# A graph layer on one core: more columns picked by VectorE and ScalarE, segments summed in half the width, and VectorE's picks placed last in each step

## The chip, the cores and the metric

The kernel runs on one core of a Trainium2 chip. The core has five engines, each with its own in-order stream of instructions: TensorE (PE, with its weight loads as PEld), VectorE (DVE), ScalarE (ACT), GpSimd (POOL) and SyncE (SP), which issues DMAs. A name with a q behind it (DVEq) means the engine's sequencer, which reads the stream and does register work itself. The metric is the device time of one execution in microseconds (us), as a median of several runs.

## The reference, cut to what matters

A graph network layer over 12,500 nodes of 128 features and 412,500 edges, sorted by target node `dst`, followed by a residual and a layer norm:

```python
f0, f1 = x0 @ W1_0e, einsum('nui,uw->nwi', x1, W1_1o)      # feat | self, scaled
e0, e1 = feat0[edge_src], feat1[edge_src]                   # gather by source node
h = gelu(gelu(edge_scalar_attr @ W_mlp1) @ W_mlp2)          # 8 -> 64 -> 64, per edge
w00, w01, w10, w11 = h @ Wp_00, h @ Wp_01, h @ Wp_10, h @ Wp_11
out0_a = w00 * e0 * ea0;            out0_b = w11 * sum(e1 * ea1)
out1_a = (w01 * e0) x ea1;          out1_b = w10 * e1 * ea0
n0, n1 = segment_sum(mid0, edge_dst), segment_sum(mid1, edge_dst)
y = c * self + s * (n0 @ W2_0e, n1 @ W2_1o)
out = layernorm(x + y)
```

All in fp32. `edge_attr_4` is (ea0, ea1), `edge_attr_8` is edge_scalar_attr.

## The kernel before, in words

Edges go in 806 runs of 512 (128 partitions, Q = 4 groups); four runs make a chunk (CH = 4), so there are 201.5 chunks. Before the main loop, the kernel turns x into `xT` (nodes along the free axis, kept in SBUF) and writes the projected features `table` to DRAM.

The rows of source nodes reach a run's tile `G` in four ways. Most are GpSimd's indirect DMAs, one for each group of 128 edges (`gather`, L194). The first RAW = 16 runs gather rows of x itself, since the table is not ready, and TensorE and ScalarE project them (`turn_rows`, `features`). Every 14th run, SP fetches one group row by row (`aid`, L184). And VectorE and ScalarE *pick*: an engine loads the node numbers of some edges as addresses into its registers (L154), then copies one column of `xT` for each (L165 on DVE, L167 on ACT) into a tile `gt`; when 128 columns are there, a matmul with `wf` (L173) and an eviction by ScalarE (L174) put them into `G`. `COLS` says how many runs one picked group takes: 5 on DVE and 7 on ACT. `gather` runs 19 runs ahead (LEAD = 20).

For each run, VectorE multiplies edge weights and gathered rows into `M` (messages, three instructions: L538 once, L541 twice). TensorE multiplies `M` by the selection `S` (32 columns: 4 attributes x 8 target nodes) into `seg`, 32 x 256 for each group (segments, L550), and ScalarE evicts all 256 columns (L553). A placing matrix `pl` (VectorE, L559, one for each run) says at which of 32 nodes of a window each segment belongs; `place` multiplies (L566 and L567), and `add` (L577) adds each run's window to the accumulator `acc` on VectorE at an offset loaded into a register (L572). `select` builds `oh` and `S` for the next chunk (L525, L529). Groups of 512 finished nodes, about one in eight chunks, go through `moments` (L594 to L607) and, two groups at a time, `normalise` (L614 to L625).

The order of PE, ACT, DVE and SP is written out by hand, in the loop over steps s at the end of the function; c, k = divmod(s, 4) are the chunk and the step in it. On VectorE a step is: messages of run s, its placing matrix, the register load and the copies of its picks; then, at k = 2, `add` for the chunk before; at k = 3 `norm` and then `select` for the next chunk; in other steps one piece of clearing (L365) if any is due. An instruction that needs a result waits on a semaphore in its place; the additions to `acc` wait for one another and S for oh.

Of the kernel before, what the change touches and what calls it, by code (L numbers as in the profile page):

```python
# [20 lines left out]
P = 128  # L21
# [15 lines left out]
LEAD = 20  # L37
RAW = 16
MARGIN = 64
# [5 lines left out]
STEPS = 12  # L45
COLS = {DVE: 5, ACT: 7}
COL_Q = {DVE: Q - 2, ACT: Q - 3}
# [5 lines left out]
def gnn_kernel(ctx: ExitStack, tc: tile.TileContext, x, src, dst, ea4, ea8, w1_0, w1_1, wm1, wm2,  # L53
# [54 lines left out]
    for e, per in COLS.items():  # L108
        picked[e], (t, k) = [], COL_TURN[e]
        while True:  # L110
            at = t + per + 1
            at += (k - at) % CH
            if at + 2 >= NS - 1:
                break
            picked[e].append((t, at, at + 2))
            t += per
    pick_of = {(e, s): i for e, g in picked.items() for i, (_, _, s) in enumerate(g)}
# [7 lines left out]
    def aid_load():  # L125


        nc.sync.dma_start(aid_at, sub(src, AID_FROM * SB + (Q - 1) * P, [[AID * SB, len(aided)], [1, P]]))
        nc.vector.tensor_scalar(aid_at, aid_at, float(4 * P), None, op0=OP.mult)
        for e, g in picked.items():  # L130
            cycle = CH // math.gcd(CH, COLS[e])
            for h in range(0, len(g), P):
                part = g[h:h + P]
                rows = cst.tile([len(part), P], I32, name=f"pick{len(pick_rows)}")
                for i in range(min(cycle, len(part))):
                    n = len(part[i::cycle])
                    nc.sync.dma_start(rows[i::cycle], sub(src, part[i][2] * SB + COL_Q[e] * P,
                                                          [[cycle * COLS[e] * SB, n], [1, P]]))
                nc.vector.tensor_scalar(rows, rows, 4.0, float(x_at), op0=OP.mult, op1=OP.add)
                for i in range(len(part)):  # L140
                    pick_rows[e, h + i] = rows[i:i + 1]
# [3 lines left out]
    def pick_nodes(e, s):  # L145

        per = COLS[e]
        i, t = divmod(s - COL_TURN[e][0], per)
        if not 0 <= i < len(picked[e]):
            return  # L150
        if t == 0:
            GT[e, i] = wk.tile([P, P], F32, name=f"gt{list(picked).index(e)}", bufs=3)
# [34 lines left out]
    def gather(s):  # L187
        b, c = divmod(s, P)
        G[s] = wk.tile([P, Q, P], F32, name="G", bufs=LEAD)
        for q in range(Q):  # L190
            if q == Q - 1 and s in aided or any(q == COL_Q[e] and (e, s) in pick_of for e in picked):
                continue
# [88 lines left out]
    wpost = cst.tile([P, 4, P], F32)  # L281
    ones = cst.tile([P, 1], F32)

    def line(dtype=F32):
# [9 lines left out]
    def clear():  # L294
        nc.vector.memset(wpost, 0.0)
        nc.vector.memset(ones, 1.0)
        nc.vector.memset(odd, 0.0)

    def weight_loads():
# [89 lines left out]

    raws = {}  # L390

    def load_raws(b):
        raws[b] = [load_run_rows(dst, b, NO_NODE), load_run_rows(src, b, 0)]

    def load_indices(b):
# [4 lines left out]
        for kind, raw in zip((1, 0), raws.pop(b)):  # L400
            f = wk.tile([P, SB], F32, name="rawf")
            nc.vector.tensor_copy(f[:ns, :], raw[:ns, :])
            if kind:
                g = wk.tile([P, SB], F32, name="rawr", bufs=1)
                off = against_window(f, g, ns)
# [14 lines left out]

    def load_run_rows(a, b, fill):
        ns = min(P, NS - b * P)
        part = b * P + ns == NS and REM < SB
        fl = ns - 1 if part else ns
        raw = wk.tile([P, SB], I32, name="raw")
        if part:
# [6 lines left out]

    e4, e8, eT, H1, H2, WP, S, M, PL, SG, ST = {}, {}, {}, {}, {}, {}, {}, {}, {}, {}, {}

    def load_edges(b):
        s0 = b * CH
        ns = min(CH, NS - s0)
        e4[b] = wk.tile([P, CH, Q, 4], F32, name="e4", bufs=EDGES_AHEAD)
        e8[b] = wk.tile([P, CH, Q, RAD], F32, name="e8", bufs=EDGES_AHEAD)  # L440
        part = s0 + ns == NS and REM < SB
        fl = ns - 1 if part else ns
        if part:
            nc.vector.memset(e4[b][:, fl], 0.0)
        if fl < CH:
            nc.vector.memset(e8[b][:, fl:], 0.0)
        for a, t, n in ((ea8, e8[b], RAD), (ea4, e4[b], 4)):
            if fl:
                nc.sync.dma_start(t[:, :fl].rearrange("p s q k -> p (s q) k"),
                                  sub(a, s0 * SB * n, [[n, P], [P * n, fl * Q], [1, n]]))  # L450
            if part and RQ:
                nc.sync.dma_start(t[:, fl, :RQ, :], sub(a, (s0 + fl) * SB * n, [[n, P], [P * n, RQ], [1, n]]))
            if part and RP:
                nc.sync.dma_start(t[:RP, fl, RQ, :], sub(a, ((s0 + fl) * SB + RQ * P) * n, [[n, RP], [1, n]]))

# [64 lines left out]
    def select(c):  # L520

        n = min(CH, NS - c * CH)
        b, r = divmod(c * CH, P)
# [3 lines left out]
                                .to_broadcast([P, n, Q, J]), op=OP.is_equal)  # L527
        S[c] = wk.tile([P, CH * Q, 4, J], F32, name="S")
        nc.vector.tensor_tensor(S[c][:, :n * Q],  # L529
                                oh[:, :n].rearrange("p s q j -> p (s q) j")[:, :, None, :]  # L530
                                .to_broadcast([P, n * Q, 4, J]),
                                e4[c][:, :n].rearrange("p s q k -> p (s q) k")[:, :, :, None]
                                .to_broadcast([P, n * Q, 4, J]), op=OP.mult)

# [10 lines left out]
    def segments(s):  # L545

        c, r = divmod(s, CH)
        pt = ps.tile([P, 2 * P], F32, name="seg", bufs=1)
        for q in range(Q):
            nc.tensor.matmul(pt[q * W:(q + 1) * W, :], S[c][:, r * Q + q].rearrange("p k j -> p (k j)"),  # L550
                             M[s][:, q].rearrange("p a u -> p (a u)"), start=True, stop=True)
        SG[s] = wk.tile([P, 2 * P], F32, name="sg", bufs=CH + 2)
        nc.scalar.activation(SG[s], pt, AF.Copy)  # L553

    def placing(s):

        b, r = divmod(s, P)
        PL[s] = wk.tile([P, P], F32, name="pl", bufs=CH + 1)
        nc.vector.tensor_scalar(PL[s], iota, colv[b][:, r:r + 1], None, op0=OP.is_equal)  # L559

    def place(c):
        ns = min(CH, NS - c * CH)
        ST[c] = pt = ps.tile([P, CH, 4, W], F32, name="m", bufs=1)
        for k in range(ns):
            s = c * CH + k
            nc.tensor.matmul(pt[:, k, 0, :], SG[s][:, :P], PL[s][:, :W], start=True, stop=True)  # L566
            nc.tensor.matmul(pt[:, k, 1:, :].rearrange("p a n -> p (a n)"), SG[s][:, P:], PL[s][:, W:],  # L567
                             start=True, stop=True)

# [12 lines left out]
    def moments(b, sums=None):  # L582
# [6 lines left out]
        pend.append(b)  # L589
        pt = ps.tile([P, XB, P], F32, name="m", bufs=1)  # L590
        st = wk.tile([P, XB, 6], F32, name="bst")
# [16 lines left out]

    def normalise():
        y, mv = Y["y"], Y["v"]  # L610
# [11 lines left out]
        for j, b in enumerate(pend):  # L622
            for t, k in group(b)[4]:
                i = j * XB + t
                nc.scalar.activation(y[:k, j, t, :], y[:k, j, t, :], AF.Identity,  # L625
                                     bias=m[:k, i:i + 1], scale=r[:k, i:i + 1])
# [3 lines left out]
    def norm(bs, last=False):  # L630
        for b in bs:
            moments(b)
            if not last:
                move_sums()
                new_sums()
            if len(pend) == LNB:
                normalise()
        if last and pend:
            normalise()

# [116 lines left out]
    with tc.manual_schedule(engines={PE, ACT, DVE, SP}):  # L757
# [7 lines left out]
        for b in range(min(3, NG)):  # L765
# [3 lines left out]
        loads = list(weight_loads())  # L769
        extra = {2: lambda: load_edges(0), 4: lambda: load_raws(0), NG // 2: lambda: load_indices(0),  # L770
                 NG // 2 + 3: make_w1b, NG // 2 + 5: make_ws, NG - 6: lambda: radial(0), NG - 4: lambda: mlp1(0),
# [36 lines left out]
        for s in range(NCH * CH + CH):  # L808
# [7 lines left out]
            if s % P == P // 2 and (s // P + 1) * P < NS:  # L816
                load_indices(s // P + 1)
            for t in range(P // ROWS):
                a = s + AID_LEAD - t * STEPS // (P // ROWS)
# [11 lines left out]
            if k == (0 if end else 1) and 0 < c <= NCH:  # L831
                place(c - 1)
            for e in picked:
                if (e, s + 2) in pick_of:
                    picked_rows(e, pick_of[e, s + 2])
            if k > 1 and c + 2 < NCH:
                pick(ACT, P)
                (mlp1 if k == 2 else mlp2)(c + 2)
            pick(ACT, P)
            pick_nodes(ACT, s + 1)  # L840
            if s + 1 < raw_runs:
                turn_rows(s + 1)
            if s < NS:
                messages(s)
                placing(s)
                pick_nodes(DVE, s)
                pick(DVE, P)
            if s + 1 < raw_runs:
# [3 lines left out]
            if k == (1 if end else 3) and 0 < c <= NCH:  # L852
                norm(due.get(c - 1, []), last=c == NCH)
                clearing += [(c, a) for a in range(4)] if c - 1 in due and c < NCH else []
            elif clearing:
                clear_sums(clearing.pop(0)[1])
            if k == 3 and c + 1 < NCH:
                select(c + 1)
            if s == NS - 8:
                count_odd()  # L860
# [31 lines left out]
```

## Time and profile before

| | |
|---|---|
| median of 10 runs | 3692.02 us (3686.87 to 3697.24) |
| the profiled execution | 3693.36 us |
| its span in the profile | 3691.6 us |
| mean granted clock of TensorE | 0.786 |
| gathers on GpSimd (L194) | 2835 from the table, 64 from x |
| picks | 20224 columns on DVE, 14336 on ACT |
| DMA | 244.14 MB, 990429 packets, 896838 of them under 512 B |

The page of the profile gives for each engine its busy time, share of the span and number of instructions, and for each group of instructions (line, engine, operation, output <- inputs, count) the busy time, the mean ns of one, the idle time just before them and what ended most of it. "issue" is idle time in which an engine waited for nothing that the profile shows. The view of waits sums the same idle times: total us, how often, longest.

### The profile page before, as it was taken

What the parts mean: (1) busy time and instruction counts of PE and PEld (TensorE: products, weight loads), DVE (VectorE), ACT (ScalarE), POOL (GpSimd) and SP (SyncE); (2) the same over time, 40 slices, a digit from 0 to 9 for tenths busy, and PEclk for the clock granted to TensorE, in tenths of its full rate; (3) what the DMA queues carried; (4) which work ended last, traced back from release to release, by engine and by line L of the source; (5) the groups of instructions that cost most, each with busy time, mean ns of one, the idle gap of its engine ahead of it and who ended that gap; (6) DMA issues with size and microseconds to landing.
All of it is one profiled execution on the core that took longest, in us unless ns stands there. A gap on an engine that the chain in (4) does not pass through costs nothing.

```text
span 3691.6 us, 117877 instructions
## 1 busy us (share of the span) xinstructions
PE 2864.8 (78%) x24857; PEld 2032.4 (55%) x24857; DVE 3062.0 (83%) x25248; ACT 2277.7 (62%) x16665; POOL 2763.7 (75%) x2906
## 2 busy tenths in 40 slices
PE   5688777778778778778778788777787877787787
PEld 4555555555555555555555455555555555555555
DVE  3698898889799888888887888878888888788886
ACT  2366676666566666666666566666566666566654
POOL 6777777777777777777777777777777777777775
PEclk8887888778778787787777777778777778777776
DMA  8233333333333333333333333333333333333331
GB/s 201 55 57 66 66 61 61 61 68 66 60 66 62 61 67 67 61 67 61 60 66 67 60 65 62 62 66 66 62 61 66 61 62 65 62 61 65 61 62 48
DMA packets 990429, 244.14 MB, mean 66 GB/s; under 512 B 896838, under 2 KB 941705, under 8 KB 989699
## 3 DMA queue, kind: packets, MB, share of 16 engines
q0 software_dynamic: 92768, 190.17, 19.3%
q1 hardware_dynamic: 876673, 39.90, 14.4%
q10 hardware_dynamic: 20258, 6.46, 0.7%
q14 instruction: 532, 4.36, 0.4%
q8 instruction: 198, 3.24, 0.4%
HBM read 223.49 MB, written 12.80 MB: 64 GB/s over the span
## 4 chain that ended last, share of the span: by engine, by line
DVE 32%; PE 15%; issue 14%; POOL 12%; DMA 9%; SPq 8%; DVEq 5%; ACT 5%; ACTq 0%; POOLq 0%
DVE gt L165 14%; POOL G L194 12%; DVE M L541 8%; DMA G<-table,idx 7%; SPq L184 5%; DVEq L154 4%; DVE M L538 3%; PE seg L550 2%; PE w L499 2%; PE m L567 2%; DVE acc L577 2%; PE m L597 2%; DVE pl L559 2%; SPq L180 2%; PE m L566 2%
## 5 line engine op out<-in xcount | busy, mean ns | idle before, releaser
L194 POOL DMA_INDIRECT G<-table,idx x2835 | 2702.2, 953 | 881.2 <-issue 734.7
L165 DVE COPY gt<-xT 128x1 f32 x20224 | 1301.6, 144 | 241.8 <-issue 230.3
L167 ACT ACTIVATE gt<-xT 128x1 f32 x14336 | 1448.4, 192 | 37.0 <-issue 34.0
L550 PE MATMUL seg<-M,S 128*32 128x256 f32 x6448 | 628.6, 468 | 489.3 <-DVE M L541 381.9
L541 DVE TENSOR_TENSOR M<-w,G 128x384 f32<-128x384 f32 x1580 | 798.6, 547 | 0.0
L499 PE MATMUL w<-wpb,h 64*128 64x128 f32 x6448 | 714.1, 355 | 106.2 <-DVE M L541 105.0
L553 ACT ACTIVATE sg<-seg 128x256 f32<-128x256 f32 x806 | 305.8, 379 | 741.4 <-PE seg L550 665.8
L499 PEld LDWEIGHTS w<-wpb,h 64*128 64x128 f32 x6448 | 591.5, 248 | 243.0 <-DVE M L541 132.6
L567 PE MATMUL m<-pl,sg 128*128 128x96 f32 x1612 | 505.3, 410 | 0.0
L550 PEld LDWEIGHTS seg<-M,S 128*32 128x32 f32 x6448 | 144.5, 118 | 624.3 <-issue 245.5
L538 DVE TENSOR_TENSOR M<-w,G 128x256 f32<-128x256 f32 x790 | 323.5, 410 | 135.4 <-DMA G<-table,idx 85.5
L566 PEld LDWEIGHTS m<-pl,sg 128*128 128x128 f32 x1612 | 358.7, 275 | 117.8 <-issue 111.6
L566 PE MATMUL m<-pl,sg 128*128 128x32 f32 x1612 | 383.9, 327 | 5.6 <-ACT sg L553 3.8
L567 PEld LDWEIGHTS m<-pl,sg 128*128 128x128 f32 x1612 | 372.3, 284 | 0.0
L482 PE MATMUL h<-h,w2b 64*64 64x256 f32 x3232 | 314.2, 403 | 51.8 <-ACT h L471 49.0
L467 PEld LDWEIGHTS h<-eT,w1b 64*128 64x128 f32 x3232 | 270.8, 250 | 148.5 <-issue 139.3
L467 PE MATMUL h<-eT,w1b 64*128 64x128 f32 x3232 | 314.9, 351 | 8.7 <-ACT eT L460 8.7
L174 ACT ACTIVATE G<-h 128x128 f32<-128x128 f32 x270 | 74.1, 274 | 345.2 <-PE h L173 303.2
L482 PEld LDWEIGHTS h<-h,w2b 64*64 64x64 f32 x3232 | 139.6, 136 | 232.2 <-ACT h L471 186.7
L577 DVE TENSOR_TENSOR acc<-m,acc 128x128 f32 x806 | 234.1, 290 | 33.6 <-PE m L567 2.4
L471 ACT ACTIVATE h<-h 128x512 f32<-128x512 f32 x404 | 217.6, 590 | 63.8 <-PE h L467 61.3
L559 DVE TENSOR_SCALAR pl<-iota,colv 128x128 f32<-128x128 f32 x806 | 236.7, 294 | 8.4 <-PE m L567 8.4
(109 smaller groups left out, 1692.4 us busy)
## 6 DMA issues: line engine op xcount, KB each, us to landing
G<-table SPq DMA_DIRECT2D x7040, 0.5 KB
G<-table,idx POOLq DMA_INDIRECT x2835
e<-in_edge_attr SPq DMA_DIRECT2D x201, 64.0 KB
e<-in_edge_attr SPq DMA_DIRECT2D x201, 32.0 KB
xt<-in_x SPq DMA_DIRECT2D x24, 256.0 KB
table<-ft ACTq DMA_DIRECT2D x24, 256.0 KB
out<-y SPq DMA_DIRECT2D x24, 256.0 KB
raw<-in_dst SPq DMA_DIRECT2D x6, 256.0 KB
```

Source lines behind the costliest of these rows:

```text
L165: nc.vector.tensor_copy(to, col)
L167: nc.scalar.activation(to, col, AF.Copy)
L194: nc.gpsimd.indirect_dma_start(out=G[s][:, q, :], out_offset=None, in_=x if s < raw_runs else table, in_offset=bass.IndirectOffsetOnAxis(a ...
L467: nc.tensor.matmul(p1[h][:, j // 2, j % 2, :], w1b[rows, j, :], eT[c][rows, :], start=True, stop=True)
L482: nc.tensor.matmul(p2[r][k * HID:(k + 1) * HID, h * n:(h + 1) * n], w2b[rows, :], H1[c][h][rows, k * n:(k + 1) * n], start=True, stop=True)
L499: nc.tensor.matmul(WP[i][:, q, :], H2[c][q % 2][rows, k, q // 2, :], wpb[rows, :], start=True, stop=True)
L538: nc.vector.tensor_tensor(m[:, :, :, :MUL], w[:, :, :2 * MUL].rearrange("p q (a u) -> p q a u", a=2), g[:, :, None, :MUL].to_broadcast([P, ...
L541: nc.vector.tensor_tensor(m[:, :, j, MUL:].rearrange("p q (i u) -> p q i u", i=3), w[:, :, None, (2 + j) * MUL:(3 + j) * MUL].to_broadcast ...
L550: nc.tensor.matmul(pt[q * W:(q + 1) * W, :], S[c][:, r * Q + q].rearrange("p k j -> p (k j)"), M[s][:, q].rearrange("p a u -> p (a u)"), s ...
L559: nc.vector.tensor_scalar(PL[s], iota, colv[b][:, r:r + 1], None, op0=OP.is_equal)
L566: nc.tensor.matmul(pt[:, k, 0, :], SG[s][:, :P], PL[s][:, :W], start=True, stop=True)
L567: nc.tensor.matmul(pt[:, k, 1:, :].rearrange("p a n -> p (a n)"), SG[s][:, P:], PL[s][:, W:], start=True, stop=True)
```

## The change

What differs, in the order of the diff:

- RAW 18 for 16; picks of one group in 4.5 runs on DVE (4 and 5 in turn) and 6 on ACT. `pick_nodes` spreads a group's 128 columns over the steps it has.
- Groups wholly past the last edge are cleared and not gathered.
- The four edge attributes come in rows of 128 edges, 2 KB each, for 32 runs at a time, and are turned by four transposes on TensorE and one eviction on ScalarE (`load_attributes`, `turn_attributes`). They came before with each chunk, 16 bytes a piece.
- `S` has 56 columns: 8 of attribute 0, 24 of zeros, 24 of attributes 1 to 3. Segments are two matmuls of 128 columns each into the same 128 columns, with columns 0 to 31 and then 24 to 55 of S. ScalarE evicts two runs in one instruction of 256 columns. `select` writes S in two instructions.
- `placing` makes the four matrices of a chunk in one instruction at k = 0; `place` is one matmul for each run.
- On VectorE the register load and copies of a step's picks come last in the step, behind `add`, `norm`, clearing and `select`. Clearing is done only at k = 1.
- `moments` uses another PSUM bank; group 0 is normalised alone, so the last pair is complete, and of that last pair every other tile is normalised by VectorE; a square root ahead of it loads ScalarE's table.
- Tiles of raw indices share other buffers.

```diff
-RAW = 16
+RAW = 18
-COLS = {DVE: 5, ACT: 7}
+COLS = {DVE: 4.5, ACT: 6}
...
     def pick_nodes(e, s):
-        per = COLS[e]
-        i, t = divmod(s - COL_TURN[e][0], per)
-        if not 0 <= i < len(picked[e]):
+        if (e, s) not in step_of:
             return
+        i, t = step_of[e, s]
+        per = len(picked[e][i][0])
...
         for q in range(Q):
+            if q * P >= E - s * SB:
+                nc.vector.memset(G[s][:, q, :], 0.0)
+                continue
...
+    def turn_attributes(b):
+        pt = ps.tile([P, 4, P], F32, name="h")
+        raw = e4_raw.pop(b).rearrange("t (e k) -> t k e", k=4)
+        for k in range(4):
+            nc.tensor.transpose(pt[:, k, :], raw[:, k, :], ident)
+        e4[b] = wk.tile([P, 4, P], F32, name="e4")
+        nc.scalar.activation(e4[b], pt, AF.Copy)
...
     def select(c):
...
-        nc.vector.tensor_tensor(S[c][:, :n * Q], ... op=OP.mult)
+        own = S_own[c % 2][:, :n * Q]
+        nc.vector.tensor_tensor(own[:, :, :J], hot, a[:, :, 0:1].to_broadcast([P, n * Q, J]), op=OP.mult)
+        nc.vector.tensor_tensor(own[:, :, W:].rearrange("p t (k j) -> p t k j", j=J),
+                                hot[:, :, None, :].to_broadcast([P, n * Q, 3, J]),
+                                a[:, :, 1:, None].to_broadcast([P, n * Q, 3, J]), op=OP.mult)
...
     def segments(s):
-        for q in range(Q):
-            nc.tensor.matmul(pt[q * W:(q + 1) * W, :], S[c][:, r * Q + q]..., M[s][:, q]..., start=True, stop=True)
-        nc.scalar.activation(SG[s], pt, AF.Copy)
+        for h, col in enumerate((0, W - J)):
+            for q in range(Q):
+                nc.tensor.matmul(SEG[c][q * W:(q + 1) * W, r, :], own[:, r * Q + q, col:col + W], M[s][:, q, h, :],
+                                 start=h == 0, stop=h == 1)
+        if r % 2 or s == NS - 1:
+            nc.scalar.activation(SG[c][:, r // 2 * 2:r + 1, :], SEG[c][:, r // 2 * 2:r + 1, :], AF.Copy)
-    def placing(s):
-        nc.vector.tensor_scalar(PL[s], iota, colv[b][:, r:r + 1], None, op0=OP.is_equal)
+    def placing(c):
+        nc.vector.tensor_tensor(PL[c][:, :n], iota[:, None, :].to_broadcast([P, n, P]),
+                                colv[b][:, r:r + n, None].to_broadcast([P, n, P]), op=OP.is_equal)
     def place(c):
-            nc.tensor.matmul(pt[:, k, 0, :], SG[s][:, :P], PL[s][:, :W], start=True, stop=True)
-            nc.tensor.matmul(pt[:, k, 1:, :]..., SG[s][:, P:], PL[s][:, W:], start=True, stop=True)
+            nc.tensor.matmul(pt[:, k]..., SG[c][:, k, :], PL[c][:, k, :], start=True, stop=True)
...
+                if last and t % 2:
+                    nc.vector.tensor_scalar(y[:k, j, t, :], y[:k, j, t, :], r[:k, i:i + 1], m[:k, i:i + 1],
+                                            op0=OP.mult, op1=OP.add)
+                    continue
-            if len(pend) == LNB:
-                normalise()
+            if len(pend) == LNB or b == 0:
+                normalise(last)
...
             if s < NS:
                 messages(s)
-                placing(s)
-                pick_nodes(DVE, s)
-                pick(DVE, P)
+                if k == 0:
+                    placing(c)
             if s + 1 < raw_runs:
                 features(s + 1)
             if k == (1 if end else 2) and 0 < c <= NCH:
                 add(c - 1)
             if k == (1 if end else 3) and 0 < c <= NCH:
                 norm(due.get(c - 1, []), last=c == NCH)
-            elif clearing:
+            elif k == 1 and clearing:
                 clear_sums(clearing.pop(0)[1])
             if k == 3 and c + 1 < NCH:
                 select(c + 1)
+            if s < NS:
+                pick_nodes(DVE, s)
+                pick(DVE, P)
```

## The prediction

> **What bounds the kernel now.** I read the busy shares first, then the waits, then the timeline of VectorE, which the chain of waits passes through most often (32%) without naming a limit.
>
> ```profile
> span 3691.6 us, 117877 instructions
> PE 2864.8 (78%) x24857; PEld 2032.4 (55%) x24857; DVE 3062.0 (83%) x25248; ACT 2277.7 (62%) x16665; POOL 2763.7 (75%) x2906
> ...
> L194 POOL DMA_INDIRECT G<-table,idx x2835 | 2702.2, 953 | 881.2 <-issue 734.7
> L165 DVE COPY gt<-xT 128x1 f32 x20224 | 1301.6, 144 | 241.8 <-issue 230.3
> ```
>
> From the waits:
>
> ```profile
> POOL G L194 <- issue: 753.9, 2472, 0.3
> ...
> DVE gt L165 <- issue: 230.3, 479, 1.7
> ...
> DVE M L538 <- DMA G<-table,idx: 85.5, 69, 6.3
> ...
> DVE M L538 <- DMA G<-table: 29.4, 7, 6.6
> ```
>
> GpSimd looks 75% busy, but its pauses are 2472 of at most 0.3 us, one behind nearly every gather: 0.95 + 0.30 us is its own rhythm. In the trace its 2899 gathers start from 3.5 to 3665.8 us, 1.264 us apart. **GpSimd is the bound.** VectorE is hardly behind: its only slack is what messages wait for gathered rows, 85.5 + 29.4 = 114.9 us. So VectorE by itself would need about 3691.6 - 114.9 = 3577 us, 3% less. Its 230 us of "issue" idle is no slack. The timeline of VectorE over one chunk of four runs (start, length, line, idle before) tells what it is:
>
> ```profile
> 1522.44 0.28 DVE L559 TENSOR_SCALAR pl<-iota,colv 128x128 f32<-128x128 f32 x1
> 1523.05 1.79 DVE L165 COPY gt<-xT 128x1 f32 x28 [0.33 <-issue]
> 1524.76 0.42 DVE L538 TENSOR_TENSOR M<-w,G 128x256 f32<-128x256 f32 x1
> 1525.09 1.01 DVE L541 TENSOR_TENSOR M<-w,G 128x384 f32<-128x384 f32 x2
> 1526.02 0.28 DVE L559 TENSOR_SCALAR pl<-iota,colv 128x128 f32<-128x128 f32 x1
> 1526.57 1.54 DVE L165 COPY gt<-xT 128x1 f32 x24 [0.27 <-issue]
> 1528.03 1.26 DVE L577 TENSOR_TENSOR acc<-m,acc 128x128 f32 x4
> 1529.20 0.41 DVE L538 TENSOR_TENSOR M<-w,G 128x256 f32<-128x256 f32 x1
> 1529.53 1.01 DVE L541 TENSOR_TENSOR M<-w,G 128x384 f32<-128x384 f32 x2
> 1530.46 0.28 DVE L559 TENSOR_SCALAR pl<-iota,colv 128x128 f32<-128x128 f32 x1
> 1531.34 1.78 DVE L165 COPY gt<-xT 128x1 f32 x28 [0.60 <-issue]
> 1533.05 0.28 DVE L525 TENSOR_TENSOR oh<-iota,rel 128x128 f32<-128x128 f32 x1
> 1533.36 0.69 DVE L529 TENSOR_TENSOR S<-oh,e 128x512 f32<-128x512 f32 x1
> ```
>
> Ahead of each group of copies the sequencer of VectorE loads their column addresses into registers (L154). The line's own view, for the time from 1529.2 to 1531.3:
>
> ```profile
> L154 DVEq TENSOR_LOAD <-pick x1: 1946/1946/1946, 1529.3 to 1529.3; - x1
> ```
>
> The copies begin 0.09 us after that load ends. Over the run a load of 24 takes 1.67 us and one of 28 takes 1.93 us, so 65 ns a register. The load costs nothing only as far as VectorE has work queued ahead of it; today that is messages and a placing matrix, 1.26 + 0.23 us.
>
> **The held sequencer.** Additions (L577) wait for one another, and S (L529) waits for oh (L525). In the trace the sequencer does nothing of its own while such an instruction waits: in none of 197 chunks does a sequencer instruction start between oh and S, and behind the last addition the next one starts 14 ns after that addition starts (197 of 198). A load put behind additions therefore begins when the fourth addition begins.
>
> The Trainium skill speaks against this: "Perfetto Trace Analysis", DVE / Act Engine Instruction, has a VectorE instruction wait in a queue of its own while the sequencer goes on. By that rule the moved load starts early and the first rival below comes true; the 14 ns above contradict it.
>
> **The change, part by part (VectorE, 201.5 chunks).**
>
> *More picks.* The built program has 2863 gathers, 36 fewer (36 x 1.264 = 45.5 us off GpSimd: 3646 if it stayed the bound), and 175 instead of 158 picks on VectorE. 17 x 128 = 2176 copies, 61 ns from start to start (four copies more are 0.24 us more in the timeline): **+133**.
>
> *Placing by chunk.* Four L559 of 0.23 us start to start go; one broadcast of 128x512 comes, which I price as L529, 0.61 us start to start. (0.61 - 0.92) x 201.5 = **-62**; between -93 (as short as L541's 0.46) and 0 (as long as the four).
>
> *Select in two pieces.* S of 0.61 us becomes 128x128 (0.23, like L559) and 128x384 (0.46, like L541): +0.08 x 201.5 = **+16**; between -30 (L541's 0.46 alone) and +62 (two of L541's, 0.92).
>
> *Clearing* moves to the second step of a chunk, whose idle (next) covers its 0.4 us, 100 times: **-41**.
>
> *Picks behind everything else.* The registers per step become 24, 28 or 32 (mean 28.4); a load takes 1.96 on average (32 by the slope: 2.19) and copies start 2.05 after the load starts. Messages occupy 1.26 us. The load usually starts 0.1 us before the messages do (median in the trace).
> - Step 0, messages and placing: copies could start at -0.10 + 2.05 = 1.95; the work ends at 1.26 + 0.61 = 1.87. Idle 0.08.
> - Step 1, messages alone: 1.95 - 1.26 = 0.69.
> - Step 2, messages and additions: these start 0.325 apart, the fourth at 1.26 + 3 x 0.325 = 2.24, and the work ends at 2.53. Load at 2.25, copies at 4.30. Idle 1.77.
> - Step 3, messages, then select: its first product starts at 1.26 + 0.32 = 1.58, the second is pushed 0.07 later, then the load: copies at 3.70; the work ends at 2.34. Idle 1.36.
>
> Sum 3.90 a chunk; 787 steps with picks are 196.75 chunks: 767 us, against 241.8 today: **+525**. All else queued on VectorE stands behind that load: the next messages, for which TensorE's segments wait, and through the freed buffers of G in the end GpSimd. Bounds of this term: with loads held nowhere it is 0.08 + 0.69 + 0.1 a chunk, 171 us, so -70; with no load running ahead of its step at all (step 0 and 1 start 0.2 us later) +600.
>
> *Moments in another bank, norm later.* L606 waits 64.5 us for ACT's copy of y; the additions are now about 1.2 us further ahead of it in each of 24 groups. Between 0 and -64; I take **-32**.
>
> *Start and end.* Twelve loads of pick indices take 9.16 us of SP; 20 are needed, +6 us, and VectorE waits for them; clearing the two S tiles about +2; the last normalise shared, with its table load ahead (1.28 us) and three pairs of tiles: -3. **+5**. 18 raw runs change little: the raw runs go at 5 us each, close to the new step.
>
> *Hidden.* TensorE sheds one of two placing matmuls a run (L566: 383.9 us) and ACT half its evictions of seg (L553: 305.8 us); in place of 16-byte pieces, attributes come in whole rows, with 4 transposes and one eviction each 32 runs. Neither engine nor the DMA engines (busy 3 tenths) set the end, so I count all at nothing. Without that cover, TensorE's new weight loads for segments (6448 more x 118 ns) are dearer by 144 us at most (L550, busy), less than it sheds. ACT gets 18 picks more at 12.9 us (1448.4 / 112); rival four.
>
> Sum: 3577 + 133 - 62 + 16 - 41 + 525 - 32 + 5 = 4121 us of span. The profiled execution took 3693.4, 1.8 more than its span, and the median of ten runs is 3692.0, so the two may be set equal: **4122 us**. A chunk then takes 20 us on VectorE against 14.2 gathers x 1.264 = 17.9 on GpSimd: the bound has passed to VectorE, and faster gathers are worth nothing.
>
> **Rivals.**
> 1. *The sequencer goes on while additions and products wait* (what would make it so: the 14 ns behind L577 being the wait of that next instruction itself). Idle is 171 us, VectorE needs 3577 + 133 - 62 + 16 - 41 - 70 - 32 + 5 = 3526, GpSimd keeps the end: 3646 + 2 = **3648, faster**. It decides if VectorE's chunk falls under 17.9, which needs over half of the 3.9 us hidden. For it: only that a pause of 14 ns is inferred, not labelled. Against: 197 of 197.
> 2. *Only one of two holds is real.* If the load gets past the additions but not past select, 1.65 us a chunk less: 4122 - 325 = **3797**. Against it: both show the same 14 ns.
> 3. *The loads are shorter than the slope says, or TensorE's relief ends small waits of VectorE*: a tenth off every load is 0.2 x 4 x 197 = 158: **3964**. Durations of one size vary only from 1.60 to 1.87, so little of that.
> 4. *ScalarE joins the chain.* It has 11.3 us busy a chunk now, 11.8 with the picks and fewer evictions, and four loads of 21 registers (1.35 each by its own 16 and 20: 1.05 and 1.29): 17.2 if nothing of them is hidden, under 20. If its waits for TensorE (0.5 to 1 us a step) add to that, a chunk becomes some 21.5: 4122 + 1.5 x 197 = **4418**.
>
> **How the numbers follow.** Forecast 84%; rival 1 7%, rival 2 3%, rival 3 as the lower end of the forecast's own range (counted in it), rival 4 5%, a change that leaves the time within 0.2% 1%. Range 3970 to 4260: from rival 3 to the forecast with loads not ahead at all (+75) and no gain at the norm or from clearing (+73); that leaves out about two in ten. 0.2% is about what measurement can tell from no change. Slower 92%, within 1%, faster 7%.
>
> **What will show it.** Right: VectorE's copies show "issue" idle near 770 us, longest in the steps behind additions (about 1.8) and select (about 1.4); pauses of GpSimd over 0.3 us become common and wait for VectorE's messages; messages wait for no gathers; L166's copies number 22400. Wrong: gathers still 1.264 us apart throughout (rival 1), or idle behind additions alone missing (rival 2), or ACT without pauses (rival 4).

## The result and the profile after

The changed kernel takes 4108.13 us (median of 8 runs, 4102.12 to 4118.56), the kernel before beside it 3692.87 us (28 runs). The ratio is 1.1127, with a 95% interval of 1.1118 to 1.1137: 415 us slower, 14 us under the forecast. The profiled execution took 4105.95 us with a span of 4104.1.

The page of the changed kernel, the same lines as before and one more (L198, L166 and L575 are L194, L165 and L538 of before):

```profile
span 4104.1 us, 131172 instructions
...
PE 2855.8 (70%) x29891; PEld 2117.8 (52%) x29891; DVE 3148.1 (77%) x27026; ACT 2410.7 (59%) x18631; POOL 2751.7 (67%) x2870
...
L198 POOL DMA_INDIRECT G<-table,idx x2791 | 2682.5, 961 | 1236.2 <-issue 772.4
L166 DVE COPY gt<-xT 128x1 f32 x22400 | 1430.1, 144 | 667.6 <-issue 656.3
...
L575 DVE TENSOR_TENSOR M<-w,G 128x256 f32<-128x256 f32 x788 | 325.9, 414 | 0.6 <-ACT G L175 0.2
```

Every engine is a smaller share of a longer span. That alone says that the time went into waiting. One copy still takes 144 ns; the idle time ahead of the copies went from 241.8 to 667.6 us, by 426, slightly more than the kernel lost. The messages, which waited 114.9 us for gathered rows, now wait 0.6 us for anything: they leave VectorE no slack. The waits (total us, times, longest) show who waits instead:

```profile
POOL G L198 <- issue: 793.5, 2516, 3.0
...
DVE gt L166 <- issue: 656.3, 515, 2.3
...
POOL G L198 <- DVE M L578: 355.5, 162, 17.0
...
DVE bst L648 <- ACT y L644: 112.0, 23, 8.1
...
PEld h L636 <- ACT h L521: 48.9, 23, 2.9
```

(The last two bear on the moments, in the section on the prediction.)

GpSimd keeps its rhythm (the median from gather to gather is 1.25 us) but stops 162 times, up to 17 us, until messages free a buffer of `G`; the mean from gather to gather becomes 1.401 us where it was 1.264. The bound has passed from GpSimd to VectorE.

VectorE's timeline in the changed kernel, the steps k = 2 and 3 of one chunk (start, length, line, idle before):

```profile
1520.98 0.41 DVE L575 TENSOR_TENSOR M<-w,G 128x256 f32<-128x256 f32 x1
1521.32 1.01 DVE L578 TENSOR_TENSOR M<-w,G 128x384 f32<-128x384 f32 x2
1522.24 1.26 DVE L619 TENSOR_TENSOR acc<-m,acc 128x128 f32 x4
1525.25 1.79 DVE L166 COPY gt<-xT 128x1 f32 x28 [1.74 <-issue]
1526.95 0.42 DVE L575 TENSOR_TENSOR M<-w,G 128x256 f32<-128x256 f32 x1
1527.28 1.01 DVE L578 TENSOR_TENSOR M<-w,G 128x384 f32<-128x384 f32 x2
1528.21 0.28 DVE L560 TENSOR_TENSOR oh<-iota,rel 128x128 f32<-128x128 f32 x1
1528.53 0.32 DVE L567 TENSOR_TENSOR S<-oh,e 128x128 f32<-128x128 f32 x1
1528.77 0.54 DVE L568 TENSOR_TENSOR S<-oh,e 128x384 f32<-128x384 f32 x1
1530.83 2.03 DVE L166 COPY gt<-xT 128x1 f32 x32 [1.52 <-issue]
```

And the view of the register load (L155) between 1522 and 1525.3 us (duration in ns, then when it starts):

```profile
L155 DVEq TENSOR_LOAD <-pick x1: 1934/1934/1934, 1523.2 to 1523.2; - x1
```

The four additions start at 1522.24 and every 0.325 us after it, so the fourth starts at 1523.2: there the load of 28 registers begins. It ends at 1525.15, and the copies start at 1525.25. VectorE's work ended at 1523.50; 1.74 us are lost in this step and 1.52 in the next.

### The profile page after: what moved, and what is told of

It is laid out like the page before. It is cut to its first block, busy times and chain, and to the rows that moved or that the text cites. A ratio compares the mean times of both kernels' runs of the same rounds, so it can differ in the third digit from the quotient of the medians.

```text
span 4104.1 us, 131172 instructions
## 1 busy us (share of the span) xinstructions
PE 2855.8 (70%) x29891; PEld 2117.8 (52%) x29891; DVE 3148.1 (77%) x27026; ACT 2410.7 (59%) x18631; POOL 2751.7 (67%) x2870
## 2 busy tenths in 40 slices
DMA packets 578334, 242.65 MB, mean 59 GB/s; under 512 B 481996, under 2 KB 526899, under 8 KB 577539
## 5 line engine op out<-in xcount | busy, mean ns | idle before, releaser
L198 POOL DMA_INDIRECT G<-table,idx x2791 | 2682.5, 961 | 1236.2 <-issue 772.4
L166 DVE COPY gt<-xT 128x1 f32 x22400 | 1430.1, 144 | 667.6 <-issue 656.3
L168 ACT ACTIVATE gt<-xT 128x1 f32 x16640 | 1662.9, 191 | 143.6 <-issue 141.8
L592 PE MATMUL seg<-M,S 128*32 128x128 f32 x12896 | 693.7, 343 | 497.5 <-DVE M L578 382.9
L592 PEld LDWEIGHTS seg<-M,S 128*32 128x32 f32 x12896 | 364.7, 129 | 697.5 <-issue 304.1
L595 ACT ACTIVATE sg<-seg 128x256 f32<-128x256 f32 x403 | 151.9, 377 | 700.9 <-PE seg L592 684.9
L610 PE MATMUL m<-pl,sg 128*128 128x128 f32 x1612 | 380.9, 410 | 1.3 <-ACT sg L595 1.3
L610 PEld LDWEIGHTS m<-pl,sg 128*128 128x128 f32 x1612 | 324.6, 299 | 69.9 <-issue 68.0
L575 DVE TENSOR_TENSOR M<-w,G 128x256 f32<-128x256 f32 x788 | 325.9, 414 | 0.6 <-ACT G L175 0.2
L619 DVE TENSOR_TENSOR acc<-m,acc 128x128 f32 x806 | 233.1, 289 | 23.5 <-PE m L610 2.1
L505 ACT ACTIVATE h<-h 128x512 f32<-128x512 f32 x404 | 216.0, 585 | 30.8 <-PE h L501 30.1
L521 ACT ACTIVATE h<-h 128x512 f32<-128x512 f32 x404 | 214.4, 581 | 14.8 <-PE h L516 9.1
L174 PE MATMUL h<-wf,gt 128*128 128x128 f32 x610 | 173.4, 382 | 7.6 <-DVE bst L648 7.6
L174 PEld LDWEIGHTS h<-wf,gt 128*128 128x128 f32 x610 | 157.2, 313 | 10.8 <-issue 10.8
```

Of the source, the lines that this page charges most:

```text
L166: nc.vector.tensor_copy(to, col)
L168: nc.scalar.activation(to, col, AF.Copy)
L174: nc.tensor.matmul(pt, GT.pop((e, i)), wf, start=True, stop=True)
L198: nc.gpsimd.indirect_dma_start(out=G[s][:, q, :], out_offset=None, in_=x if s < raw_runs else table, in_offset=bass.IndirectOffsetOnAxis(a ...
L575: nc.vector.tensor_tensor(m[:, :, :, :MUL], w[:, :, :2 * MUL].rearrange("p q (a u) -> p q a u", a=2), g[:, :, None, :MUL].to_broadcast([P, ...
L592: nc.tensor.matmul(SEG[c][q * W:(q + 1) * W, r, :], own[:, r * Q + q, col:col + W], M[s][:, q, h, :], start=h == 0, stop=h == 1)
```

## The experiments

The theory: VectorE's sequencer works strictly in order, and the load of the picks' registers takes it some 2 us a step. The load costs nothing as far as VectorE still has work to do that was handed to it (pushed) before the load began. Behind additions and selections, which wait for one another, the load starts too late to be hidden; **the order** makes the time. The rivals: the rest of the change (2176 more copies, the bank of the moments, the start) makes it; or the load alone, wherever it stands.

The first four kernels of this section ran where the kernel before took 3694 to 3697 us.

**The order undone (e1b).** The changed kernel, with load and copies back behind messages and placing.

```diff
                 if k == 0:
                     placing(c)
+                pick_nodes(DVE, s)
+                pick(DVE, P)
...
-            if s < NS:
-                pick_nodes(DVE, s)
-                pick(DVE, P)
```

> The changed kernel with VectorE's register load and copies back behind the messages and placing matrices, ahead of additions, norm, clearing and select. Theory (a load costs what no queued work of VectorE covers, and holds all behind it): idle before copies 0.1, 0.35, 0.35 and 0.85 us in the four steps (the load of step 3 begins when the last addition does, 0.1 after the messages begin), 320 us in all against 668, and clearings uncovered, +40: 4108 - 348 + 40 = 3800 (3740 to 3830). Rival (not the order but narrower segments, split select or more picks cost): above 4050.

Measured: 3725.70 us, 1.0069 [1.0048, 1.0091] of before. Two lines of the order give back 382 of the 415 us. The page's line of the copies, and the timeline of VectorE in step 3 of a chunk, with the additions of step 2 just ahead of it:

```profile
L166 DVE COPY gt<-xT 128x1 f32 x22400 | 1433.3, 144 | 306.2 <-issue 296.4
```

```profile
1515.59 0.41 DVE L575 TENSOR_TENSOR M<-w,G 128x256 f32<-128x256 f32 x1
1515.92 1.01 DVE L578 TENSOR_TENSOR M<-w,G 128x384 f32<-128x384 f32 x2
1518.07 2.03 DVE L166 COPY gt<-xT 128x1 f32 x32 [1.14 <-issue]
```

As many copies of the same length, 361 us less idle ahead of them. What is left comes mostly in the steps behind additions (0.84 us in step 3): the additions still end the step before, and the next load still waits for the fourth of them. The time came out 74 us below the 3800 expected, and under the range. By the account of VectorE in the table below, the copies' idle is 13 us less than expected, the statistics wait 36 us less, and the 40 us put down for uncovered clearing did not come; busy time and other waits take 17 back.

**The order alone (e2b).** The kernel before, with only its load and copies moved behind additions, norm, clearing and selection.

```diff
                 messages(s)
                 placing(s)
-                pick_nodes(DVE, s)
-                pick(DVE, P)
...
             if k == 3 and c + 1 < NCH:
                 select(c + 1)
+            if s < NS:
+                pick_nodes(DVE, s)
+                pick(DVE, P)
```

> The kernel before with the order alone: register load and copies last in the step, all else as before. Theory: the load (1.77 us for 25.6 registers) begins at the fourth addition, 2.48 after the messages begin, and at S, 1.82 after; idle 1.58 and 1.19 us in steps 2 and 3 and 0.17 in the other two, 3.1 a chunk or 614 us against 242: 3577 + 372 = 3950 (3900 to 4010). Rival (the order matters only with the changed segments or more picks): 3693 to 3720.

Measured: 3970.45 us, 1.0745 [1.0727, 1.0763]: 273 us slower with no other part of the change, as expected. The idle ahead of the copies is 657.0 us, as in the changed kernel. The timeline shows the same picture, with the placing matrices of before as cover:

```profile
1504.38 1.25 DVE L577 TENSOR_TENSOR acc<-m,acc 128x128 f32 x4
1507.13 1.69 DVE L165 COPY gt<-xT 128x1 f32 x24 [1.50 <-issue]
```

So the order is enough for most of the loss, without any other part of the change. The rival that the rest of the change makes the time is out.

**Only the load early (e3b).** The changed kernel, its load behind messages and placing, its copies still last. If only the load's late start counts, the additions now run beside it.

```diff
                 if k == 0:
                     placing(c)
+                pick_nodes(DVE, s)
...
             if s < NS:
-                pick_nodes(DVE, s)
                 pick(DVE, P)
```

> The changed kernel with the register load alone moved ahead, behind the messages, and the copies last in the step, taken once more: on the chip of the first call the kernel before itself took 5550 us instead of 3692, since all engines got their instructions late, so that what this kernel tells was covered up. Theory as before: the idle of steps 2 and 3 goes (358 + 249 us), VectorE needs about 3500 and GpSimd sets the end: 3650 (3640 to 3690). Rival (it is the place of the copies that costs): no better than 4050. Second rival (registers held for longer stall the sequencer): between the two.

Measured: 3807.51 us, 1.0300 [1.0283, 1.0317]. Faster than the changed kernel, but not what was expected. The timeline of a step with additions, and two groups (the last number before the arrows is the idle time ahead of them):

```profile
1500.53 1.01 DVE L578 TENSOR_TENSOR M<-w,G 128x384 f32<-128x384 f32 x2
1502.79 1.27 DVE L619 TENSOR_TENSOR acc<-m,acc 128x128 f32 x4 [1.25 <-issue]
1503.98 2.02 DVE L166 COPY gt<-xT 128x1 f32 x32
```

```profile
L619 DVE TENSOR_TENSOR acc<-m,acc 128x128 f32 x806 | 235.3, 292 | 221.8 <-PE seg L592 98.5 <-issue 54.7 <-PE h L501 43.9
L560 DVE TENSOR_TENSOR oh<-iota,rel 128x128 f32<-128x128 f32 x202 | 58.8, 291 | 71.8 <-issue 70.7
```

The copies hardly wait any more (57.4 us); the additions do (221.8 against 23.5), and so do `oh` (71.8 against 0) and clearing (46.9 against 5.4). The expectation had the additions run while the load runs. They don't: they stand behind it in the same stream, and in none of the 787 loads of picks does an addition, `oh`, `S` or a clearing start before the load has ended. The idle moved to whatever comes next. The theory had to be widened: a load is hidden only by work that stands *ahead* of it and takes long once pushed (messages do; additions, held until the last has started, don't). The releasers named for L619, TensorE's segments, are put down by the profile; of the 202 groups of additions 111 wait over 1 us here, and one in each of the other kernels of this section and in the kernels before and after.

The wait ahead of additions is more than the rest of that load. They have a small register load of their own (L614, the offsets in `acc`). In the changed kernel it ends 1.1 us before the additions start (median); here it starts right behind the load of the picks, 0.07 us after its end (median). Both loads of the step shown above (duration in ns, then when it starts):

```profile
L155 DVEq TENSOR_LOAD <-pick x1: 2099/2099/2099, 1499.8 to 1499.8; - x1
```

```profile
L614 DVEq TENSOR_LOAD <-first_at x1: 571/571/571, 1502.0 to 1502.0; - x1
```

VectorE's work ended at 1501.54, the picks' load at 1501.94, the additions' own at 1502.59. Over the run, 62 us of the idle ahead of the first additions lie before the picks' load has ended and 138 behind it. `oh` and clearing have no load of their own and show the plain hold.

The second rival of the expectation (registers held for longer) named the range that came true, but its reason does not show: a load of 32 takes 2.19 us here and 2.18 in the changed kernel, and the loads of steps 2 and 3 start 0.36 us ahead of the messages (median).

**All but the order (e7).** The order undone, and three more parts: a placing matrix for each run behind its messages, clearing between messages and load, and the moments back in the bank that `place` uses, as before. The edit is shown against e1b.

```diff
-        PL[c] = wk.tile([P, CH, P], F32, name="pl")
-        nc.vector.tensor_tensor(PL[c][:, :n], ... op=OP.is_equal)
+        if k == 0:
+            PL[c] = wk.tile([P, CH, P], F32, name="pl")
+        nc.vector.tensor_scalar(PL[c][:, k], iota, colv[b][:, r:r + 1], None, op0=OP.is_equal)
...
-        pt = ps.tile([P, XB, P], F32, name="h")
+        pt = ps.tile([P, XB, P], F32, name="m", bufs=1)
...
-                if k == 0:
-                    placing(c)
+                placing(s)
+                if k == 1 and clearing:
+                    clear_sums(clearing.pop(0)[1])
                 pick_nodes(DVE, s)
...
```

> The changed kernel with the order undone, a placing matrix for each run again behind its messages (so that the load has 0.23 us more to hide under in steps 1 to 3), clearing between messages and load, and the moments in the bank that place uses. Theory: idle 0.05, 0.25, 0.25 and 0.6 us a chunk, VectorE at about 3720, less some 60 that moments now wait for ScalarE's second gelu: 3660, next to GpSimd's 3646; 3645 to 3720, a little under the 3693 of before. Rival (GpSimd's or ScalarE's further picks cost by themselves): 3740 and more.

Measured: 3692.98 us, 0.9987 [0.9977, 0.9996]: in the range, but 33 us above the 3660 expected and as long as before. From its page:

```profile
L198 POOL DMA_INDIRECT G<-table,idx x2791 | 2657.0, 952 | 874.5 <-issue 728.4
```

Cover ahead of the load brings the idle of the copies to 256.8 us, near the 241.8 of before, though there are 2176 more of them. GpSimd is back at a mean of 1.266 us, with 20 gathers that start over 1.6 us behind the one ahead (35 before), and its last gather starts at 3625.7 us. Before, that was 3665.8, with 26 us to the end; now 68 us follow. So GpSimd, with 36 gathers fewer, does end earlier, and VectorE, with its additional copies, takes what was won. The cover as such won nothing over e1b: by the table, VectorE is 50 us longer busy for 49 us less idle ahead of copies. Of the 30 us between the spans of the two kernels 26 are the statistics.

One account of VectorE serves all five kernels. From the 3577 us that VectorE needed before without its waits for gathered rows, to each span (us; idle is that ahead of the named instructions; the other waits are what remains):

| | after | e1b | e2b | e3b | e7 |
|---|---|---|---|---|---|
| busy time | +86 | +90 | -17 | +76 | +140 |
| idle, copies | +426 | +64 | +415 | -184 | +15 |
| idle, additions, oh, clearing | -10 | -3 | -10 | +301 | -5 |
| idle, statistics (L648) | +57 | +22 | +36 | +63 | -4 |
| other waits of VectorE | -32 | -26 | -32 | -23 | -29 |
| span less 3577 | +527 | +147 | +392 | +233 | +117 |

The parts add up: the rest without the order is +147, the order alone +392, together 539, and the whole change is +527. Against the span of before they seem not to add (+32, +277, +412), because each of the two by itself uses up the same 114.9 us of slack. This says where VectorE's time went; of the parts other than the order only the three that e7 takes back were run without the rest.

**Four other chips.** Eight runs fell on chips where the kernel before itself took 5466 to 5550 us, so that they can be compared with nothing above:

| | us | beside the kernel before |
|---|---|---|
| e1_order_undone, as e1b | 5630.29 | 1.0135 [1.0091, 1.0179] |
| e2_order_alone, as e2b | 5523.35 | 0.9949 [0.9928, 0.9969] |
| e3_load_early, as e3b | 5511.29 | 0.9926 [0.9900, 0.9952] |
| e4_load_early_at_add | 5548.10 | 0.9992 [0.9972, 1.0013] |
| e9_five_six | 5487.57 | 1.0043 [1.0023, 1.0063] |
| e9b_five_six | 5562.06 | 1.0039 [1.0022, 1.0056] |
| e9c_five_six | 5578.08 | 1.0056 [1.0029, 1.0082] |
| e10_five_five | 5549.50 | 1.0125 [1.0086, 1.0164] |

> The changed kernel with one thing undone: VectorE's register load and copies stand again behind the messages (and the placing matrices), ahead of additions, norm, clearing and select. Theory (a load is held by the additions and by select's first product, and VectorE then sets the end): the idle of 1.82 and 1.27 us a chunk in steps 2 and 3 falls to some 0.35 each, 668 us of idle before copies become about 220, and the clearings, no longer under that idle, cost some 40: 4108 - 445 + 40 = about 3700, between 3650 (GpSimd's own rate, 2863 x 1.264) and 3740. Rival (the order is not what costs; narrower segments, split select or more picks are): it stays above 4050.

> The kernel before with the order alone: register load and copies last in the step, all else as before. Theory: the load (1.77 us for 25.6 registers) begins at the fourth addition, 2.48 after the messages begin, and at S, 1.82 after; idle 1.58 and 1.19 us in steps 2 and 3 and 0.17 in the other two, 3.1 a chunk or 614 us against 242: 3577 + 372 = 3950 (3900 to 4010), with VectorE as the bound. Rival (the order matters only with the changed segments or with more picks): 3693 to 3720.

> The changed kernel with the register load alone moved ahead, behind the messages; the copies stay last in the step. Theory: the load runs under additions or select, the idle of steps 2 and 3 goes wholly (358 + 249 us), VectorE needs about 3500 and GpSimd sets the end again: 3650 (3640 to 3690). Rival (it is the place of the copies that costs, since messages, and TensorE behind them, wait for them): no better than 4050. Second rival (registers held for longer stall the sequencer): between the two.

e4 moves the load ahead of the additions at k = 2 alone; its idle ahead of the copies of that step is 0.0 us, and 1.34 us in step 3:

```diff
+                if k == 2:
+                    pick_nodes(DVE, s)
...
-                pick_nodes(DVE, s)
+                if k != 2:
+                    pick_nodes(DVE, s)
```

> The changed kernel with the register load moved ahead of the additions, in step 2 of a chunk alone. Theory: only the 358 us behind additions go, those of select stay: 4108 - 358 = 3750, a chunk of 18.0 us on VectorE against GpSimd's 17.9, so 3750 to 3800 where the two meet. Rival (only select holds the load): 4108. Rival (only additions hold it): idle behind select is not 1.27 us a chunk, and the time is under 3700.

e9, e9b and e9c are one kernel, e7 with as many picks on VectorE as before, and e10 also takes more on ScalarE, to see whether a version between the two beats both:

```diff
-COLS = {DVE: 4.5, ACT: 6}
+COLS = {DVE: 5, ACT: 6}
```

> The last kernel (order undone, placing for each run, moments in place's bank) with VectorE's picks back at one group in 5 runs, ScalarE's left at 6. Theory: that kernel is bound by VectorE, whose last message comes 47 us after the last gather; 17 picks less take 133 us off it and shorter loads some 50, so GpSimd sets the end: 2880 gathers x 1.266 + 3 + some 25 behind the last = 3672 (3660 to 3690), under the 3693 of before. Rival (VectorE isn't what binds it, GpSimd's rate is): 17 gathers more cost 21 us, 3715.

> The kernel with the order undone, placing for each run, moments in place's bank, and picks of one group in 5 runs on VectorE and 6 on ScalarE, taken once more, since on the chip of the last call all engines got their instructions late. Theory as before: VectorE loses 133 us of copies and some 50 of loads, GpSimd sets the end: 2880 gathers x 1.266 + 3 + some 25 behind the last = 3672 (3660 to 3690), under the kernel before. Rival (GpSimd's rate binds that kernel already): 17 gathers more cost 21 us, 3715.

> The same kernel a third time (order undone, placing for each run, moments in place's bank, picks of one group in 5 runs on VectorE and 6 on ScalarE), the last chip too having given all engines their instructions late. Theory: 3672 (3660 to 3690) on a chip where the kernel before takes 3695, a ratio of 0.994. Rival (GpSimd's rate binds the kernel with 4.5 already): 3715, 1.006.

> The same with ScalarE picking one group in 5 runs too. Theory: if ScalarE has the time, 2854 gathers x 1.266 + 28 = 3640 (3630 to 3665). Rival: ScalarE has 11.9 us busy a chunk already, 13.6 with 27 picks more, and four loads of 26 registers at 1.67 us; if these are not hidden, a chunk is 20 us against 17.7, and the time is 3900 or more.

(e10 has {DVE: 5, ACT: 5}.) Whether 5 and 6 would beat before where the kernel before takes 3695 us stays open: it was not measured there. Nor were the bank of the moments alone and fewer picks on the changed kernel with its own order.

## Why the prediction was right

The mechanism was the one forecast, and the sum came within 17 us of the span, 4121 against 4104.1. Its terms, one by one, by the table's first column:

- **Picks, placing, selection: right in sum.** +133 - 62 + 16 = +87; VectorE's busy time grew by 86. The copies number 22400.
- **The late load: right in kind, and in the two steps that carry it.** Steps 0 to 3 were put at 0.08, 0.69, 1.77 and 1.36 us; they are 0.08, 0.20, 1.82 and 1.27. The load starts 2.242 us after the messages do in step 2 (median; 5 to 95%: 2.235 to 2.250; predicted 2.25), and the copies at 4.34 in the mean (4.30). In step 3 it starts at 1.591 (median; predicted 1.65). A load of 24 takes 1.67 us, of 28 1.93, of 32 2.18 (2.19 by the slope).
- **Step 1 was mis-sized.** The load starts 0.30 us ahead of the messages, not 0.1, which leaves 0.35 us without clearing; with clearing, half of the time, 0.035. The term of clearing (-41) was right in what it said, that this idle hides it (0.32 us of its 0.4), but both terms together were -41 + 525 = +484 and came to +426.
- **The moments: wrong in sign.** Predicted -32, measured +57. The step that failed was "the additions are now about 1.2 us further ahead of it". VectorE does come to the statistics later, 4.70 us after the additions end with the order alone, where it was 3.74 (medians of 25 groups), but TensorE starts the moments later still: 3.24 us after the additions instead of 0.16, straight from other matmuls (its median pause there is 0). The head start was counted as if TensorE were free. The order alone, with the old bank, has the statistics waiting 100.1 us instead of 64.5; the rest without the order 86.0; both 121.5, which adds the two rises. What the rest adds is likely the bank: the statistics (L648) wait for ScalarE's copy, that for TensorE's matmuls, and the first of these (L636) waits for ScalarE's gelu (L521), 48.9 us at its weight load, in the changed kernel and 50.2 in e1b, which have the new bank. Before, in e2b and in e7, which have the old one, it never does, and in e7 the statistics wait 60.3 us. But e7 differs from e1b in placing and clearing too.
- **Start and end: no +5.** The first messages start at 111.6 us against 111.9, so the eight more loads of pick indices delayed nothing there; from the start of the last messages to the end it is 19.7 us against 21.0.
- **A term was missing.** VectorE's other small waits, messages' and placing's for TensorE and ScalarE above all, ended with the slack, and the additions wait 10 us less: -42 together. As VectorE became the bound, it found most inputs ready. 3577 was therefore too much by these.
- **Hidden: right.** TensorE is busy 70%, ScalarE 59%; no wait of VectorE on either grew but the one above. TensorE's weight loads for segments cost more than the "144 us at most": they went from 144.5 to 364.7 us of busy time, still without setting the end. DMA packets fell from 990429 to 578334; the account of VectorE needs no term for them.

The errors are -58, +89, -5, -42, and they nearly cancel; that the sum is within 17 us is luck, though its largest term, the late load with clearing, was right to 58 us. Two slips in the working: the upper end adds up to 4270, not 4260; and over all 202 groups of additions in the kernel before, the next instruction of the sequencer starts 13 to 19 ns behind the start of the last addition in 189, where the prediction has 197 of 198. In the others it starts later, which does not speak against the hold. The rivals: the load does not run ahead of additions (rival 1) nor of selection (rival 2), as 2.242 and 1.591 us show; ScalarE (rival 4) waits 684.9 us for segments and does not set the pace. The Trainium skill has a VectorE instruction wait in a queue of its own while the sequencer goes on ("Perfetto Trace Analysis", DVE / Act Engine Instruction); this trace disagrees, by those same two numbers.

## What to carry to other kernels

Ask of every register load what work stands ahead of it on its own engine that is already pushed and waits for nothing, and look at what stands behind it as well: here moving load and copies behind instructions that wait cost 382 us, though the 2 us of the load never became longer. Cover that has to be made for the purpose can cost what it hides (e7). Price a change from what each engine needs, not from the span: parts that use up the same slack do not add in the span, but here they nearly added (539 against 527) in that account. Before work is taken off the engine that bounds (36 gathers here), look at how little the next one has left: VectorE had 3%.

## What was not expected of the hardware

In these traces a register load holds all that stands behind it, not only the copies that use its registers: with the load ahead of it, `oh`, which uses no register, waited 71.8 us in all, where it waited for nothing before (e3b).

On the four chips with 5466 to 5550 us, single instructions take what they take elsewhere (145 ns a copy in e3_load_early), but they come singly. VectorE's timeline of e2_order_alone within one group of copies:

```profile
2007.29 0.28 DVE L165 COPY gt<-xT 128x1 f32 x3 [0.46 <-issue]
2008.01 0.15 DVE L165 COPY gt<-xT 128x1 f32 x1 [0.44 <-issue]
2008.75 0.21 DVE L165 COPY gt<-xT 128x1 f32 x2 [0.59 <-issue]
```

In e3_load_early VectorE stands idle for over 150 ns between two copies of one group 1765 times, 1085 us in all; in the changed kernel's trace 13 times, 3 us. SyncE's register moves, 29 ns in the median on all chips, reach 702 ns at the 95th percentile there and 29 on the others. TensorE's idle that the profile puts down to nothing is 696 us in e3_load_early and 2 us in the changed kernel. So the streams of these three engines are late; that this is why the order of VectorE's own work decides little there is likely, not tested. What delays them is not shown.
